# Weighting the experts' blocks two passes ahead, and fewer slots between the routing's steps

## The chip, the cores and the metric

The kernel runs on one core of one Trainium2 chip. The metric is the device time of one execution in microseconds (us), lower is better. The profile is of one execution on that core, taken by the hardware profiler; its time axis starts with the first instruction. Engines are named as the profile does: PE is TensorE (PEld its weight loads), DVE is VectorE, ACT is ScalarE, POOL is GpSimd, SP is SyncE, whose queue here issues most of the DMAs.

## The reference

Two layers run over x of shape (8, 384, 32, 32) in float32. Layer 0 adds a state space block (group norm, layer norm, projection, a short convolution, a selective scan over 1024 tokens with 16 states, gate, projection, and an MLP with Gelu). Layer 1, the one that the change touches, adds a mixture of four experts, and every expert is computed for every token:

```python
x_flat = x.transpose(0, 2, 3, 1).reshape(-1, c)
scores = softmax(x_flat @ gate_w + gate_b, -1)
top_v, top_i = jax.lax.top_k(scores, 2)
top_w = softmax(top_v, -1)
wmap = top_w.T.reshape(2, b, h, w)
present = (top_i[:, :, None] == jnp.arange(e)[None, None, :]).any(0)   # (2, E)
coef = jnp.einsum('ke,kbhw->ebhw', present, wmap)
hdn = relu(einsum('bchw,edc->ebdhw', x, w1) + b1)
y = einsum('ebdhw,eod->ebohw', hdn, w2) + b2
out = einsum('ebohw,ebhw->bohw', y, coef)          # x = x + out
```

Here x is the group-normed output of layer 0. `present` looks over all tokens at once: an expert counts as present at rank k if any token anywhere chose it there. So no coefficient is known before the last token has its scores. The second layer of an expert is linear, so the kernel may weight the hidden block by the coefficient ahead of it, and add coefficient times b2 to the sum.

## The kernel before

The tokens are cut into 16 chunks (`NCH`) of 512 (`T`); the 384 channels are 3 slabs (`J`) of 128 partitions. A hidden block of one expert and one chunk is 128 x 3 x 512.

**The first 3400 us** are the scan of layer 0 (loop L985), into which a planner fits everything else: the projections, the MLP, the scores of finished chunks, and the first expert layer (`expert_lane`, L606), which puts relu blocks through ACT into DRAM (`r_dram`).

**The planner.** All such work is written as generators that yield (engine, cost, wait). `wait` is the number of slots that must pass before the step after the yield may be issued; `Task.resume` (L792) sets `ready` to the current slot plus wait. `issue` (L801) takes ready steps by urgency (rank times 6, plus ready) until none is left. A step on "bank" also needs one of four PSUM banks, counted in `held`; an `evict` task frees it two slots later. The order in which the planner issues is the order of each engine's queue: each engine then works its queue off in that order, waiting on semaphores. In `drain` (L859) every slot issues all that is ready. So while the expert layer runs in a drain, a slot is worth some blocks of six matmuls (L619) on PE and as many evictions (L623) on ACT.

**The routing** (`route`, L629) starts when all 16 chunks have their logits (`logged`). It runs over all 64 token tiles at once, in steps, each after a yield with a wait: bias, maximum and subtraction on DVE (L649 to L651); Exp on ACT (L653); a long DVE step of softmax and of two rounds of picking the best (L655 to L679); a second Exp (L681) and its normalization (L683 to L685); a matmul over the counts, which is `present` (L690); the coefficients on DVE (L693 to L698); two transposes on PE (L705); a copy on ACT (L709); and two DMAs into `coef_dram` (L712). After the scan, `second_layers` (L867) begins `last_x1` and `route` with rank 0, ahead of all else, and drains until `routed`; then it fetches the coefficients of chunk 0 (L910) and drains the rest, which is the end of the first expert layer for the last chunk. Weight tiles of that layer come through `Stream`, three buffers, loaded by SP two blocks ahead (L218).

**The second expert layer** is the loop L913, one pass for each chunk and expert, 64 in all. There is no planner here: the order is that of the code. A pass tops up the list `ahead` of hidden blocks in flight (pool `phid`, six buffers, L894), at a chunk's first expert loads the next chunk's x1 (`load_sum`, L890, three buffers) and its coefficients, the same on all partitions (`load_coef`, L882, pool `pc`, two buffers, tile `spread`), and takes three accumulators, from `ps_acc` for even chunks and from the banks for odd ones. It multiplies the hidden block by its coefficients on DVE (L922), issues nine matmuls on PE (L925; each fp32 matmul is two instructions in the trace, so 18, and 72 for a chunk), and adds coefficient times bias to x1 on DVE, once for each slab (L928). At a chunk's last expert, `expert_out` (L897) adds the three accumulators to x1 on DVE (L900) and writes the result (L901). DVE and SP work strictly through what the passes have given them, so the first L922 of a chunk stands behind the three L900 of the chunk before.

Of the kernel before, what the change touches and what calls it, by code (L numbers as in the profile page):

```python
# [11 lines left out]
F32 = mybir.dt.float32  # L12
# [6 lines left out]
P = 128  # L19
B, C, L = 8, 384, 1024  # L20
T = 512
NH = L // T
NCH = B * NH
J = C // P
# [22 lines left out]
def chunk_of(dram, i):  # L47

    b, h = divmod(i, NH)
    return dram[b].rearrange("(p j) (n s) w -> n p j (s w)", p=P, n=NH)[h]  # L50


def wide(ap, shape):
    return ap.to_broadcast(shape)
# [56 lines left out]
def layers(ctx, tc, io, ident, cmean, eps, dram, x1_dram, gn1, logits, r_dram, group_norm):  # L111
# [9 lines left out]
    def pool(name, bufs, stack=ctx, **kw):  # L121
        return stack.enter_context(tc.tile_pool(name=name, bufs=bufs, **kw))
# [75 lines left out]
    def bank(name):  # L198
        held[0] += 1
        return ps_g.tile([P, T], F32, name=name, tag="g")  # L200

    def free():
        held[0] -= 1
# [394 lines left out]
    def last_x1(pool):  # L598
        while NCH - 1 not in scored:
            yield "-", 0, 1  # L600
        yield from normal_x1(NCH - 1, pool.tile([P, J, T], F32, name="last_xn"))
# [29 lines left out]
    def route(pool):  # L631
        while len(logged) < NCH:
            yield "-", 0, 1
        names = iter(range(99))

        def part(*shape):
            return pool.tile([P, *shape], F32, name=f"route{next(names)}")

        def over_experts(ap):
            return wide(ap.unsqueeze(2), [P, NT, E])  # L640

        def over_tiles(ap):
            return wide(ap.unsqueeze(1), [P, NT, E])

        yield "DVE", 2, 1
        ones = part(P)
        G.memset(ones, 1.0)
        sc, m = part(NT, E), part(NT)
        V.tensor_tensor(sc, logits, over_tiles(gate_b), ALU.add)  # L649
        V.tensor_reduce(m, sc, AX.X, ALU.max)  # L650
        V.tensor_tensor(sc, sc, over_experts(m), ALU.subtract)  # L651
        yield "ACT", 0.4, 2
        S.activation(sc, sc, AF.Exp)  # L653
        yield "DVE", 10, 0
        V.tensor_reduce(m, sc, AX.X, ALU.add)  # L655
        V.reciprocal(m, m)
        V.tensor_tensor(sc, sc, over_experts(m), ALU.mult)

        top = []
        count = part(2, E)  # L660
        for k in range(2):
            best = part(NT)
            V.tensor_reduce(best, sc, AX.X, ALU.max)
            pick = part(NT, E)
            V.tensor_tensor(pick, sc, over_experts(best), ALU.is_equal)

            left = part(NT)
            V.tensor_scalar(left, pick[:, :, 0], -1.0, 1.0, ALU.mult, ALU.add)
            for e in range(1, E):
                V.tensor_tensor(pick[:, :, e], pick[:, :, e], left, ALU.mult)  # L670
                V.tensor_tensor(left, left, pick[:, :, e], ALU.subtract)
            V.tensor_reduce(count[:, k, :], pick.rearrange("p t e -> p e t"), AX.X, ALU.add)
            if k == 0:
                V.scalar_tensor_tensor(sc, pick, -2.0, sc, ALU.mult, ALU.add)
            top.append(best)


        w_hi, w_lo = part(NT), part(NT)
        V.tensor_tensor(w_lo, top[1], top[0], ALU.subtract)  # L679
        yield "ACT", 0.3, 3  # L680
        S.activation(w_lo, w_lo, AF.Exp)  # L681
        yield "DVE", 1, 0
        V.tensor_scalar(w_hi, w_lo, 1.0, None, ALU.add)  # L683
        V.reciprocal(w_hi, w_hi)
        V.tensor_tensor(w_lo, w_lo, w_hi, ALU.mult)  # L685


        yield "bank", 0.2, 1
        total = bank("total")
        PE.matmul(total[:, 0:2 * E], lhsT=ones, rhs=count.rearrange("p k e -> p (k e)"), start=True, stop=True)  # L690
        yield "DVE", 1, 1
        present = part(2, E)
        V.tensor_scalar(present.rearrange("p k e -> p (k e)"), total[:, 0:2 * E], 0.5, None, ALU.is_gt)  # L693
        free()
        coef = part(NT, E)
        V.tensor_tensor(coef, over_experts(w_hi), over_tiles(present[:, 0, :]), ALU.mult)
        V.tensor_tensor(sc, over_experts(w_lo), over_tiles(present[:, 1, :]), ALU.mult)
        V.tensor_tensor(coef, coef, sc, ALU.add)  # L698


        half = NT // 2
        yield "bank", 0.4, 1
        ct = bank("ct")
        for k in range(2):
            PE.transpose(ct[:, k * P:(k + 1) * P], coef[:, k * half:(k + 1) * half, :].rearrange("p t e -> p (t e)"),  # L705
                         ident)
        yield "ACT", 0.4, 1
        cs = part(2, P)
        S.copy(cs, ct[:, 0:2 * P].rearrange("p (k n) -> p k n", k=2))  # L709
        free()  # L710
        for k in range(2):
            nc.sync.dma_start(coef_dram[k * half:(k + 1) * half].rearrange("t e s -> (t e) s"), cs[:, k, :])  # L712
        routed.append(True)
# [6 lines left out]
    def at(r):  # L720
        i, k = divmod(r, per)
        return i, *divmod(k, NG)
# [75 lines left out]
    def begin(*new, rank=2):  # L798
        tasks.extend(Task(t, rank) for t in new)
# [59 lines left out]
    def drain(until=lambda: not tasks):  # L859
        while not until():  # L860
            credit.update(PE=99, ACT=99, DVE=99, batch=99)
            issue(everything)
            slot[0] += 1
        credit.update(PE=0, ACT=0, DVE=0)


    def second_layers():  # L867
        def weight(name, shape):
            t = we.tile(shape, F32, name="w_" + name)
            nc.sync.dma_start(t, io[name])  # L870
            return t

        we, po, pc, px, phid = pool("we", 1), pool("po", 2), pool("pc", 2), pool("px", 3), pool("phid", 6)
        ps_acc = pool("ps_acc", 4, space=PSUM)
        todo = [(i, e) for i in range(NCH) for e in range(E)]
        spread = {}

        def load_coef(i):
            if i < NCH:
                spread[i] = pc.tile([P, TT, E, P], F32, name="spread")  # L880
                mine = coef_dram[i * TT:(i + 1) * TT]
                nc.sync.dma_start(spread[i].rearrange("p t e s -> p (t e s)"),  # L882
                                  mine.rearrange("t e s -> (t e s)").partition_broadcast(P))

        x2 = {}

        def load_sum(i):
            if i < NCH:
                x2[i] = px.tile([P, J, T], F32, name="x1")
                nc.sync.dma_start(x2[i], x1_dram[i])  # L890

        def load_hidden(n):
            (i, e), r = todo[n], phid.tile([P, J, T], F32, name="r")
            nc.sync.dma_start(r, r_dram[i][e * J:(e + 1) * J].rearrange("j p t -> p j t"))  # L894
            return r

        def expert_out(i, acc):  # L897
            o = po.tile([P, J, T], F32, name="o")
            for j in range(J):
                V.tensor_tensor(o[:, j, :], acc[j], x2[i][:, j, :], ALU.add)  # L900
            nc.sync.dma_start(chunk_of(io["out"], i), o)  # L901
            del x2[i]

        ahead = deque(load_hidden(n) for n in range(2))
        e2 = weight("e_w2", [P, E, J, J, P])
        eb2 = weight("e_b2", [P, E, J])
        load_sum(0)
        begin(last_x1(we), route(we), rank=0)
        drain(lambda: routed)
        load_coef(0)  # L910
        drain()

        for n in range(len(todo)):  # L913
            while len(ahead) < 4 and n + len(ahead) < len(todo):
                ahead.append(load_hidden(n + len(ahead)))
            (i, e), r = todo[n], ahead.popleft()
            if e == 0:
                load_sum(i + 1)
                load_coef(i + 1)
                acc = [ps_acc.tile([P, T], F32, name="acc") if i % 2 == 0 else bank("acc") for _ in range(J)]  # L920
            r4 = r.rearrange("p j (t s) -> p j t s", s=P)
            V.tensor_tensor(r4, r4, wide(spread[i][:, :, e, :].unsqueeze(1), [P, J, TT, P]), ALU.mult)  # L922
            for d in range(J):
                for j in range(J):
                    PE.matmul(acc[j], lhsT=e2[:, e, d, j, :], rhs=r[:, d, :], start=(e + d == 0), stop=(e + d == E + J - 2))  # L925
            for j in range(J):
                x4 = x2[i][:, j, :].rearrange("p (t s) -> p t s", s=P)
                V.scalar_tensor_tensor(x4, spread[i][:, :, e, :], eb2[:, e, j:j + 1], x4, ALU.mult, ALU.add)  # L928
            if e == E - 1:
                expert_out(i, acc)  # L930

    with tc.manual_schedule():
# [52 lines left out]
        for r in range(rounds):  # L985
            i, d, s = at(r)
# [75 lines left out]
```

## Time and profile before

| | |
|---|---|
| time, median of 3 runs (lowest to highest) | 4132.92 us (4128.94 to 4134.43) |
| time of the profiled execution | 4128.67 us |
| its span, first to last instruction | 4126.9 us |
| PE busy, share of the span | 3707.8 us, 90% |
| DVE busy | 3029.4 us, 73% |
| ACT busy | 2423.1 us, 59% |
| POOL busy | 2780.4 us, 67% |
| mean granted clock of TensorE | 0.951 |
| second expert layer, first matmul to the end of the last | 3576.34 to 4121.48 us |
| in it: PE busy, DVE busy, ACT busy | 508.3, 264.7, 0 us |
| DMA, mean over the span | 161 GB/s |

How it is read: a row of the timeline gives the start, the duration, the engine, the line of the kernel, the operation, what it writes and reads, how often, and in brackets how long the engine sat idle ahead of it and what ended that. The chain is followed back from the last instruction to what released each step, so time outside it did not set the end. Ends of matmuls are modelled, since they are pipelined: the start-to-start distance of weight loads is the surer measure of the pace. A granted clock of 1.00 is full speed.

### The profile page before, as it was taken

Reading aid. Unit: us, or ns where it says so; the run is one execution under the profiler, and the core shown is the slowest. Engines: PE = TensorE matmul, PEld = TensorE weight load, DVE = VectorE, ACT = ScalarE, POOL = GpSimd, SP = SyncE. Lnnn points to the kernel's source line nnn. Section 1 sums busy time; section 2 is a strip of 40 time slices with the busy share of each in tenths; the row PEclk is TensorE's granted clock in tenths of the full one; section 3 lists DMA queues with packets and bytes.
Section 4 is the critical chain, followed back from the end, with each engine's and each line's share of the span. In section 5 each row is a group of like instructions: output and inputs, shape, how many; then the busy total and the mean of one; then the engine's idle time right before and its main releaser. Section 6 shows DMA issues by size and latency. Waiting matters only on the chain. (4 is left out here: it accounts for less than half of the span.)

```text
span 4126.9 us, 35165 instructions
## 1 busy us (share of the span) xinstructions
PE 3707.8 (90%) x10294; PEld 1383.3 (34%) x10294; DVE 3029.4 (73%) x3081; ACT 2423.1 (59%) x3762; POOL 2780.4 (67%) x1070
## 2 busy tenths in 40 slices
PE   6678888999999999998999999999998998899998
PEld 2123223333333333333333333333333333344443
DVE  4888888888887888888878787888787770244444
ACT  4757676767676768676767676768666753100000
POOL 3898988788878888888888888888788860000000
PEclk8779898999999999999999999999999998999999
DMA  4434445464546454555455545554555443544443
GB/s 130 139 132 129 162 131 164 143 199 156 185 138 197 167 171 152 187 175 166 143 186 174 172 146 189 174 172 153 172 167 173 154 153 116 174 169 171 170 170 127
DMA packets 372499, 665.31 MB, mean 161 GB/s; under 512 B 40252, under 2 KB 151228, under 8 KB 370132
## 3 DMA queue, kind: packets, MB, share of 16 engines
q1 hardware_dynamic: 342496, 612.38, 44.8%
q10 hardware_dynamic: 29812, 50.68, 3.2%
q8 instruction: 83, 1.36, 0.1%
q14 instruction: 108, 0.88, 0.1%
HBM read 535.90 MB, written 127.01 MB: 161 GB/s over the span
## 5 line engine op out<-in xcount | busy, mean ns | idle before, releaser
L739 POOL TENSOR_TENSOR du<-dxr,b 128x2048 f32<-128x2048 f32 x384 | 1738.9, 4528 | 23.6 <-PE y L773 13.1
L751 POOL TENSOR_TENSOR du<-du,c 128x1024 f32<-128x1024 f32 x384 | 906.0, 2359 | 227.5 <-DVE du L747 202.2
L731 ACT ACTIVATE da_A<-dtr_a,w_a_log 128x512 f32<-128x512 f32 x768 | 527.6, 687 | 282.6 <-DVE du L751 123.1
L731 ACT ACTIVATE da_B<-dtr_b,w_a_log 128x512 f32<-128x512 f32 x768 | 527.3, 687 | 263.4 <-DVE du L747 210.7
L479 PE MATMUL hid<-tt,mlp_w 128*128 128x512 f32 x1152 | 535.9, 607 | 63.8 <-ACT h L483 46.7
L773 PE MATMUL y<-du,sel 128*32 128x512 f32 x3072 | 467.2, 641 | 130.2 <-DVE du L751 84.4
L747 DVE TENSOR_TENSOR_SCAN du<-da_B,carry,du 128x512 f32<-128x512 f32 x384 | 488.2, 1271 | 117.8 <-ACT da_B L731 109.9
L296 PE MATMUL g_in<-xt,in_proj 128*128 128x512 f32 x1152 | 556.8, 621 | 15.5 <-DVE x L523 8.4
L619 PE MATMUL e_hid<-xn,e_w 128*128 128x512 f32 x1080 | 517.9, 626 | 47.0 <-ACT r L623 25.7
L518 PE MATMUL acc<-h,mlp_w 128*128 128x512 f32 x1152 | 539.8, 611 | 22.4 <-ACT h L494 14.4
L747 DVE TENSOR_TENSOR_SCAN du<-da_B,du 128x512 f32<-128x512 f32 x384 | 464.5, 1210 | 122.1 <-ACT da_B L731 105.0
L925 PE MATMUL acc<-r,w_e_w 128*128 128x512 f32 x1152 | 508.3, 603 | 45.3 <-DVE r L922 40.3
L747 DVE TENSOR_TENSOR_SCAN da_A<-da_A,carry,du 128x512 f32<-128x512 f32 x384 | 489.1, 1274 | 8.6 <-ACT da_A L731 8.1
L747 DVE TENSOR_TENSOR_SCAN da_A<-da_A,du 128x512 f32<-128x512 f32 x384 | 465.5, 1212 | 27.6 <-ACT da_A L731 26.0
L751 DVE TENSOR_TENSOR du<-da_A,c 128x1024 f32<-128x1024 f32 x384 | 470.2, 1225 | 13.2
L479 PEld LDWEIGHTS hid<-tt,mlp_w 128*128 128x128 f32 x1152 | 213.9, 192 | 364.0 <-issue 236.3
L925 PEld LDWEIGHTS acc<-r,w_e_w 128*128 128x128 f32 x1152 | 221.6, 194 | 331.4 <-issue 277.5
L518 PEld LDWEIGHTS acc<-h,mlp_w 128*128 128x128 f32 x1152 | 215.5, 194 | 340.2 <-issue 247.9
L296 PEld LDWEIGHTS g_in<-xt,in_proj 128*128 128x128 f32 x1152 | 210.5, 194 | 354.0 <-issue 254.3
L619 PEld LDWEIGHTS e_hid<-xn,e_w 128*128 128x128 f32 x1080 | 207.0, 198 | 347.0 <-issue 247.9
L457 PE MATMUL g_out<-xc,out_proj 128*128 128x512 f32 x576 | 279.1, 632 | 32.0 <-DVE xc L780 32.0
L408 POOL TENSOR_TENSOR dtx<-dt,xc 128x512 f32<-128x512 f32 x96 | 122.1, 1272 | 209.9 <-DVE dt L405 209.8
(129 smaller groups left out, 3033.4 us busy)
## 6 DMA issues: line engine op xcount, KB each, us to landing
dxr<-dxr_dram SPq DMA_DIRECT2D x384, 256.0 KB, 4.8
mlp_w<-in_mlp_w SPq DMA_DIRECT2D x384, 192.0 KB, 3.2
dtr_b<-dtr_dram SPq DMA_DIRECT2D x192, 256.0 KB, 3.9
dtr_a<-dtr_dram SPq DMA_DIRECT2D x192, 256.0 KB, 3.2
r_dram<-r ACTq DMA_DIRECT2D x192, 256.0 KB, 3.3
r<-r_dram SPq DMA_DIRECT2D x64, 768.0 KB, 8.0
in_proj<-in_in_proj SPq DMA_DIRECT2D x192, 192.0 KB, 3.6
e_w<-in_e_w SPq DMA_DIRECT2D x192, 192.0 KB, 3.2
```

Source lines behind the costliest of these rows:

```text
L296: PE.matmul(g, lhsT=w[:, j, :], rhs=xt[i][:, j, :], start=(j == 0), stop=(j == J - 1))
L408: G.tensor_tensor(dtx, dt, xc[i, d], ALU.mult)
L457: PE.matmul(g, lhsT=w[:, d, :], rhs=xc[i, 3 * k + d], start=(k + d == 0), stop=(k == 1 and d == 2))
L479: PE.matmul(g, lhsT=w[:, j, :], rhs=tt[i][:, j, :], start=(j == 0), stop=(j == J - 1))
L518: PE.matmul(g, lhsT=w[:, n, :], rhs=hs[mine[n]], start=(k + n == 0), stop=(k == 1 and n == 2))
L619: PE.matmul(h, lhsT=w[:, j, :], rhs=xn[:, j, :], start=(j == 0), stop=(j == J - 1))
L731: S.activation(out, dtr[i, d][pair][:, j % 2, :], AF.Exp, scale=neg_a[:, d, j, s:s + 1])
L739: G.tensor_tensor(du[r], dxr[i, d], wide(bt[i, s].unsqueeze(1), [P, Q, T]), ALU.mult)
L747: V.tensor_tensor_scan(a if j < 2 else b, a, b, start, ALU.mult, ALU.add)
L751: engine.tensor_tensor(du[r][:, js, :], h, wide(ct[i, s].unsqueeze(1), [P, 2, T]), ALU.mult)
L773: PE.matmul(y[j * m:(j + 1) * m, :], lhsT=sel, rhs=h[:, j, :], start=False, stop=(s == NG - 1), tile_position=(0, j * m), skip_group_check ...
L925: PE.matmul(acc[j], lhsT=e2[:, e, d, j, :], rhs=r[:, d, :], start=(e + d == 0), stop=(e + d == E + J - 2))
```

## The change

In `route`, four waits become shorter by a slot each: the first DVE step 1 to 0 slots, the first Exp 2 to 1, the second Exp 3 to 2, the step on `total` 1 to 0. (The other waits stay.) In the second expert layer, what stood at the head of a pass, from topping up `ahead` to the weighting, becomes a function `weigh(n)`. It is called for passes 0 and 1 ahead of the loop, and for pass n + 2 in pass n, after the additions L928 and ahead of `expert_out`. The loads that hang on a chunk's first expert move with it. The accumulators are still taken in the pass that first uses them.

```diff
-        yield "DVE", 2, 1
+        yield "DVE", 2, 0
...
-        yield "ACT", 0.4, 2
+        yield "ACT", 0.4, 1
         S.activation(sc, sc, AF.Exp)
...
-        yield "ACT", 0.3, 3
+        yield "ACT", 0.3, 2
         S.activation(w_lo, w_lo, AF.Exp)
...
         PE.matmul(total[:, 0:2 * E], lhsT=ones, rhs=count.rearrange("p k e -> p (k e)"), start=True, stop=True)
-        yield "DVE", 1, 1
+        yield "DVE", 1, 0
         present = part(2, E)
...
-        for n in range(len(todo)):
+
+        weighted = {}
+
+        def weigh(n):
+            if n >= len(todo):
+                return
             while len(ahead) < 4 and n + len(ahead) < len(todo):
                 ahead.append(load_hidden(n + len(ahead)))
             (i, e), r = todo[n], ahead.popleft()
             if e == 0:
                 load_sum(i + 1)
                 load_coef(i + 1)
-                acc = [ps_acc.tile([P, T], F32, name="acc") if i % 2 == 0 else bank("acc") for _ in range(J)]
             r4 = r.rearrange("p j (t s) -> p j t s", s=P)
             V.tensor_tensor(r4, r4, wide(spread[i][:, :, e, :].unsqueeze(1), [P, J, TT, P]), ALU.mult)
+            weighted[n] = r
+
+        weigh(0)
+        weigh(1)
+        for n, (i, e) in enumerate(todo):
+            r = weighted.pop(n)
+            if e == 0:
+                acc = [ps_acc.tile([P, T], F32, name="acc") if i % 2 == 0 else bank("acc") for _ in range(J)]
             for d in range(J):
                 for j in range(J):
                     PE.matmul(acc[j], lhsT=e2[:, e, d, j, :], rhs=r[:, d, :], start=(e + d == 0), stop=(e + d == E + J - 2))
             for j in range(J):
                 x4 = x2[i][:, j, :].rearrange("p (t s) -> p t s", s=P)
                 V.scalar_tensor_tensor(x4, spread[i][:, :, e, :], eb2[:, e, j:j + 1], x4, ALU.mult, ALU.add)
+            weigh(n + 2)
             if e == E - 1:
                 expert_out(i, acc)
```

## Prediction

> **What bounds the kernel now.** I read four views. The chain that ended last, in order of time, comes first: it tells which of the changed lines set the end at all. The routing and the expert loop are its last part.
>
> ```profile
> 3557.26 10.40 PE e_hid L619 x24
> 3568.31 1.55 DMA coef_dram<-route
> 3569.87 4.53 DMA spread<-coef_dram
> 3574.53 1.77 DVE r L922
> 3576.34 33.18 PE acc L925 x72
> 3609.52 2.50 issue
> 3612.02 31.15 PE acc L925 x72
> 3643.80 1.76 DVE r L922
> 3645.60 32.69 PE acc L925 x72
> ```
>
> Columns: start, length, engine, tile, line. From 3576.34 to 4121.48 us the chain is TensorE on the 16 chunks (72 matmuls each), and between any two of them one weighting (L922) or an "issue" of the same length. Ahead of it stands the end of the routing: TensorE is done with e_hid at 3567.7 and idle until the coefficients are in DRAM, back on the chip, and the first block is weighted. Second, the timeline of VectorE at one boundary (start, length):
>
> ```profile
> 3641.48 0.69 DVE L900 TENSOR_TENSOR o<-acc,x 128x512 f32<-128x512 f32 x1 [16.61 <-PE acc L925]
> 3642.34 0.69 DVE L900 TENSOR_TENSOR o<-acc,x 128x512 f32<-128x512 f32 x1 [0.17 <-PE acc L925]
> 3643.19 0.69 DVE L900 TENSOR_TENSOR o<-acc,x 128x512 f32<-128x512 f32 x1 [0.17 <-PE acc L925]
> 3643.80 1.75 DVE L922 TENSOR_TENSOR r<-r,spread 128x1536 f32<-128x1536 f32 x1
> ```
>
> VectorE had been idle for 16.61 us, at the head of its queue an addition that waits for the accumulators. The next chunk's first weighting stands behind the additions, so TensorE waits for it. Third, the weight loads of TensorE after this boundary, and the windows of this chunk and the one before:
>
> ```profile
> 3645.60 0.50 PEld L925 LDWEIGHTS acc<-r,w_e_w 128*128 128x128 f32 x2 [3.28 <-DVE r L922]
> 3646.62 0.34 PEld L925 LDWEIGHTS acc<-r,w_e_w 128*128 128x128 f32 x1 [0.52 <-issue]
> ```
>
> ```profile
> 3612.00:3645.60 33.60, 31.14 (x72) 13.58 (x72) 16.66 (x20) 0.00 (x0) 0.00 (x0) 1.00 0.46 172
> 3645.60:3680.80 35.20, 32.70 (x73) 14.29 (x73) 16.75 (x20) 0.00 (x0) 0.00 (x0) 0.96 0.44 165
> ```
>
> After this gap a load takes 0.34 instead of 0.19 us and the pitch is 0.86 instead of 0.43: half clock, for some 3.4 us. The second window (columns: length, busy time of PE, PEld, DVE, ACT and POOL, then the granted clock, DMA share, GB/s) is 1.6 us longer, at clock 0.96. Fourth, the timeline of the routing:
>
> ```profile
> 3527.39 0.69 ACT L623 ACTIVATE r<-e_hid,w_e_b 128x512 f32<-128x512 f32 x1 [1.89 <-PE e_hid L619]
> 3536.20 0.42 ACT L653 ACTIVATE route<-route 128x256 f32<-128x256 f32 x1 [0.40 <-ACT r L623]
> 3545.68 0.26 ACT L681 ACTIVATE route<-route 128x64 f32<-128x64 f32 x1 [9.06 <-DVE route L679]
> 3546.57 10.57 PE L619 MATMUL e_hid<-last_xn,e_w 128*128 128x512 f32 x24 [1.19 <-ACT r L623]
> 3556.97 0.28 PE L690 MATMUL total<-route,route 128*128 128x8 f32 x2
> 3567.49 0.38 PE L705 MATMUL ct<-ident,route 128*128 128x128 f32 x2
> ```
>
> VectorE had the scores ready at 3521.4, but the first Exp ran at 3536.20: the planner had put it behind that many evictions. The transposes L705 stand behind the last e_hid block.
>
> [...] The half-clock stretches here start at 3645.60, 3747.99, 3850.36, 3952.75 and 4055.14, that is 102.4 us apart, [...] gaps of 2.45 us trip it, 5 of 15. [...]
>
> **The change, part by part.** All sums are against the profiled execution: 4128.67 us, span 4126.9, so 1.8 us lie around it. The median of the runs shown is 4132.92, 4.25 higher; I subtract from that.
>
> *1. Weighting two ahead.* No instruction is added: 64 weightings of 1.749 us and 192 additions of 0.744 us (L928) stay. A chunk's first two blocks are now weighted in the third and fourth pass of the chunk before, the second of them ahead of the additions L900. TensorE then has two blocks (18 matmuls each, 15.4 us) without VectorE. Behind the additions stand three L928 and a weighting (2.1 + 1.75 us), which are due 15.4 us after the boundary and done some 5.5 us after it: 10 us of cover. Start to start, an undisturbed chunk now takes 33.61 us (3612.02 to 3645.60); 72 matmuls at the steady pitch of the weight loads, 0.429 us, take 30.9. So a boundary costs 2.71[...], 15 of them 40.7 us.
>
> *2. Half clock.* Without gaps nothing trips it. The five long chunks take 35.15 instead of 33.61: 5 x 1.54 = 7.7 us. The first chunk takes 35.68, 2.07 more, after its 8.46 us of idle: gone as well if part 3 fills that. The stage goes from 545.1 (3576.34 to 4121.48) to 16 x 30.9 + 0.25 = 494.7: 50.5 us, the sum of the three.
>
> *3. Routing.* I follow the planner by hand; in the drain a slot issues all that is ready, and four banks bound the e_hid blocks. Counting from the slot in which the last logits are copied (0): before, the first VectorE step is in slot 2, the first Exp in 4, the second in 7, "total" tried in 8 and placed in 9 after eight blocks of the last chunk, transposes in 11 after all twelve, the copy in 12. That is the order the trace shows. After: VectorE step in 1, Exp in 2, second Exp in 4, "total" and the coefficients in 5, ahead of the last chunk's first block, transposes in 7 after its fourth, copy and the write of coef_dram in 8.
> Exp then runs behind the eviction of 3527.39, at about 3528.5, 7.7 us sooner; VectorE's 9 us of picks end at 3545.5 - 7.7 = 3537.8. "total" needs them, and TensorE reaches it at 3534.9, the end of the chunk before: a **new stall** of 3.0 us with all e_hid blocks queued behind it. In exchange the stall of 1.19 us at 3546.57 goes, for which the second Exp held ScalarE. Twelve blocks then run from 3538.1: 72 x 0.429 = 30.9, transposes 0.4, end 3569.4. Idle 3.0 us may trip the half clock: between 0 and 1.6, I take 0.8.
> On SP, in order, the write of coef_dram stands behind the weights of block 8, which wait for block 5's buffer: 3554. It lands 1.6 later; behind block 9's weights (3556.5) the coefficients are fetched: 4.5 us by the chain, 8.8 by the median landing of that row, so 3561 to 3565.4, and two weightings end at 3569 at the latest. The first is done by 3567.2, ahead of TensorE. If this cover failed, each us is one on the path. Weights of blocks 10 and 11, behind that fetch, are issued at 3559 and 3562, land 3.2 later, are used at 3564 and 3567: 2 us in hand.
> So the expert matmuls start at 3569.4 + 0.8 instead of 3576.3: 6.1 us.
>
> *4. Queues and buffers.* With each chunk's first weighting its loads move two blocks forward: x1 of the chunk after (a third buffer, free) and its spread. Spread has two buffers, and the older is read once more by L928 of the fourth block, so SP waits there until VectorE has passed it; VectorE runs ahead of TensorE, and that costs SP a few us. A block of r is now asked for five ahead in six buffers, so it waits for the block before the running one: 7.7 us each, landing 8.0, but four blocks early. The output's DMA holds SP until the additions are over, as before; the next r behind it is due over 20 us later. I take nothing for all this; if the cover were gone, a late r would cost up to its 8.0 us landing per chunk.
>
> Sum: 50.5 + 6.1 = 56.6 us. 4132.9 - 56.6 = **4076.3**; a profile near 4072.
>
> **The rivals.**
> - *The coefficients are late all the same* (one of the fetches or the stall is longer): part 3 gives nothing and the first chunk's 2.07 stay: 4132.9 - 48.4 = 4084.5. Against it: 2 us or more in hand. Chance 0.09.
> - *The half clock isn't tied to the gaps*: the 7.7 and 2.1 stay: 4086. For it: a period of 102.4 us. Against it: every stretch starts at the end of a gap, and three chunks make 102.4 as well. Chance 0.07.
> - *Another wait steps into the boundary* (spread or r after SP's new waits), half of the 40.7 stay, and of the 7.7: 4100. Chance 0.07.
> - *Transfers become the bound, slower.* A chunk moves 4 r, x1, spread and out: 5.77 MB. At 30.9 us that asks 187 GB/s; undisturbed chunks now move 172. If SP's waits let only the span's mean of 161 through, a chunk takes 35.8 us, the stage 573, and 4132.9 + 28 - 6 = 4155. It decides from 34.4 us per chunk (168 GB/s) on. Against it: 199 GB/s in a slice of the page, DMA shares under 0.5 in this stage. At 172 it would end near 4123. Chance 0.04.
> - *The change doesn't do what it says*: the planner would have to place the steps otherwise, or the old buffers hold the weighting back: 4133. Chance 0.01.
>
> **How the numbers follow.** The forecast has 0.72; its own spread is the half clock (0 to 1.6), the coefficients, and the 4 us between profile and median: 4070 to 4081. To 4087 the first two rivals are in: 0.88, less a little at the edges. Hence 4070 to 4087. A measurement of this kernel tells 0.2% (8 us) from no change; faster by more holds for all but the last two rivals: 0.95, same 0.02, slower 0.03.
>
> **What would show it.** Right: in the chain one run of acc matmuls without L922, chunk pitch 30.9, clock 1.00 throughout; L922 ahead of L900 on VectorE; Exp near 3528.5; "total" ahead of the last e_hid blocks, with some 3 us of idle before it; no idle before the first acc. Wrong: idle of TensorE with r, spread or x as releaser in the stage, half-clock loads with no gap before them, or a pitch over 31 us.

## The result and the profile after

| | before | after |
|---|---|---|
| median time, us (lowest to highest, runs) | 4131.88 (4128.94 to 4134.43, 4) | 4077.61 (4072.95 to 4086.60, 4) |
| span of the profiled execution | 4126.9 | 4073.9 |
| first DVE step of the routing (L649) to the end | 606.8 | 551.1 |
| second expert layer, first matmul to the end of the last | 545.1 | 494.6 |

The ratio of the times is 0.9872, 95% interval 0.9853 to 0.9890: 1.3% faster, 54.3 us (45 to 61 by the interval). The forecast was 4076.3 us, which is 56.6 us less.

The third row needs a word. Up to L649 no instruction is changed, yet the ten profiles of this study reach it between 3512.0 and 3531.7 us. Executions of one kernel scatter nearly as much: 15 runs of the kernel before spread over 15.2 us. This scatter is larger than some of the effects below. So each profile is measured from its own L649 to its end. There the change saves 55.8 us; the spans, 53.0 us apart, hold 2.8 us of that scatter.

The end of the chain that ended last, after (start, length, engine, tile, line, count):

```profile
3541.14 12.10 PE e_hid L619 x24
3553.46 20.60 PE e_hid L619 x48
3574.06 494.41 PE acc L937 x1152
4068.50 0.69 DVE o L900
```

All 16 chunks are one unbroken run of TensorE, 1152 matmuls of 0.429 us; no weighting and no "issue" stands between them, and e_hid runs straight into them. (The timeline, which the table uses, counts this run from its first start, 3573.90, and gives it 494.56 us.) VectorE at the first boundary, in the timeline of after:

```profile
3587.90 1.75 DVE L926 TENSOR_TENSOR r<-r,spread 128x1536 f32<-128x1536 f32 x1
...
3603.28 0.69 DVE L900 TENSOR_TENSOR o<-acc,x 128x512 f32<-128x512 f32 x1 [13.63 <-PE acc L937]
3604.14 0.69 DVE L900 TENSOR_TENSOR o<-acc,x 128x512 f32<-128x512 f32 x1 [0.17 <-PE acc L937]
3605.00 0.69 DVE L900 TENSOR_TENSOR o<-acc,x 128x512 f32<-128x512 f32 x1 [0.17 <-PE acc L937]
3605.61 2.07 DVE L940 SCALAR_TENSOR_TENSOR x<-spread,w_e_b,x 128x512 f32<-128x512 f32 x3
...
3607.59 1.75 DVE L926 TENSOR_TENSOR r<-r,spread 128x1536 f32<-128x1536 f32 x1
```

VectorE still idles ahead of the additions (13.63 us here), but the next chunk's second weighting starts over 15 us before them. The weighting behind them ends at 3609.3, and its block is the third of the new chunk, which TensorE reaches some 11 us later. The windows (length, busy time of PE, PEld, DVE, ACT and POOL, granted clock, DMA share, GB/s) show the clock and the traffic:

```profile
3600.00:3700.00 100.00, 100.00 (x234) 44.31 (x233) 53.77 (x63) 0.00 (x0) 0.00 (x0) 1.00 0.51 180
3700.00:3800.00 100.00, 100.00 (x234) 44.28 (x233) 57.39 (x66) 0.00 (x0) 0.00 (x0) 1.00 0.54 189
```

TensorE is busy throughout, at clock 1.00; the DMA engines carry 180 to 189 GB/s in about half of their time. The routing, in the timeline of after:

```profile
3530.18 0.69 ACT L623 ACTIVATE r<-e_hid,w_e_b 128x512 f32<-128x512 f32 x1 [1.89 <-PE e_hid L619]
3531.33 0.42 ACT L653 ACTIVATE route<-route 128x256 f32<-128x256 f32 x1 [0.46 <-ACT r L623]
3540.78 0.36 PE L690 MATMUL total<-route,route 128*128 128x8 f32 x2 [2.92 <-DVE route L679]
3541.00 12.24 PE L619 MATMUL e_hid<-last_xn,e_w 128*128 128x512 f32 x24
3553.08 0.38 PE L705 MATMUL ct<-ident,route 128*128 128x128 f32 x2
3561.64 0.38 SPq L882 DMA_DIRECT2D spread<-coef_dram  x1
3567.54 3.43 DVE L926 TENSOR_TENSOR r<-r,spread 128x1536 f32<-128x1536 f32 x2 [24.08 <-DMA r_dram<-r]
```

Exp runs 8.5 us after L649, where it took 16.1 before. The count matmul L690 now stands ahead of the last chunk's twelve blocks, and TensorE waits 2.92 us for the picks (L679) that it needs. The 24 matmuls behind it take 12.24 us instead of some 10.4. Both weightings of the first blocks end by 3570.97, 2.9 us ahead of TensorE at 3573.90. (The last row names a write of r to DRAM as releaser, which the weighting does not read. Of what it does read, the spread was fetched last, at 3561.64, 5.9 us earlier.)

### The profile page after: what moved, and what is told of

It reads as the page before. It is cut to its first block, busy times and chain, and to the rows that moved or that the text cites. A ratio compares the mean times of both kernels' runs of the same rounds, so it can differ in the third digit from the quotient of the medians.

```text
span 4073.9 us, 35181 instructions
## 1 busy us (share of the span) xinstructions
PE 3697.5 (91%) x10294; PEld 1383.9 (34%) x10294; DVE 3030.1 (74%) x3081; ACT 2422.4 (59%) x3762; POOL 2779.7 (68%) x1070
## 5 line engine op out<-in xcount | busy, mean ns | idle before, releaser
L937 PE MATMUL acc<-r,w_e_w 128*128 128x512 f32 x1152 | 494.6, 592 | 0.0
```

## The experiments

The explanation to be tested has three parts: the breaks of TensorE at 15 boundaries (40.7 us), the half clock that some of them set off (7.7 us), and the gap ahead of the stage (the rest). In the table, "from L649" is the profile's time from there to the end, and "saved" is against before's 606.8. There is one profile of each kernel, so these have no interval; but after, e3 and e4, whose TensorE does the same work in the same order, agree to 0.5 us. The ratio of after is to the 4 runs of the kernel before shown above, those of e1 to e4 are to 15 further runs of it (median 4130.97), and those of e5 to e8 to 7 (4129.23).

| kernel | median, us | ratio, 95% interval | from L649, us | saved, us |
|---|---|---|---|---|
| after | 4077.61 | 0.9872 (0.9853 to 0.9890) | 551.1 | 55.8 |
| e1_loop_only | 4079.83 | 0.9883 (0.9858 to 0.9908) | 558.3 | 48.6 |
| e2_route_only | 4128.43 | 0.9989 (0.9978 to 1.0000) | 600.3 | 6.5 |
| e3_one_ahead | 4075.50 | 0.9872 (0.9857 to 0.9887) | 551.5 | 55.3 |
| e4_adds_first | 4074.07 | 0.9866 (0.9850 to 0.9883) | 551.1 | 55.7 |
| e5_by_slab | 4106.24 | 0.9950 (0.9935 to 0.9965) | 582.7 | 24.2 |
| e8_bias_first | 4180.97 | 1.0127 (1.0112 to 1.0142) | 661.2 | -54.4 |
| e6_total_later | 4073.20 | 0.9869 (0.9849 to 0.9890) | 548.6 | 58.3 |
| e7_coef_act | 4074.68 | 0.9875 (0.9860 to 0.9890) | 547.4 | 59.4 |

**The two halves of the change.** e1 is the kernel after with the four old waits, e2 the kernel before with the four new ones:

```diff
 e1, against after (e2, against before, has the same four lines the other way)
-        yield "DVE", 2, 0
+        yield "DVE", 2, 1
...
-        yield "ACT", 0.4, 1
+        yield "ACT", 0.4, 2
...
-        yield "ACT", 0.3, 2
+        yield "ACT", 0.3, 3
...
-        yield "DVE", 1, 0
+        yield "DVE", 1, 1
```

> The new expert loop with the routing's old waits. Theory (boundaries 40.7 us, half clock 7.7 us, routing the rest): the stage keeps its idle of 8.5 us ahead of the first matmul and the slow first chunk (2.1 us), then runs at a pitch of 30.9 us; 48.4 us saved, 4083.5 us. Rival (the earlier coefficients are what lets the loop run ahead): waits for r or spread in the first chunks, over 4090 us.

> The shorter waits with the old expert loop. Theory: the gap of 8.5 us ahead of the stage goes, a stall of 2.9 us at the count matmul comes, the first chunk runs at full clock; the 15 boundaries stay as they were: 5.1 + 2.1 = 7 us saved, 4125 us. Rival (routing worth nothing, its gain is given back): 4132 us.

The timeline of TensorE in e1 has the stage as one row:

```profile
3568.37 496.45 PE L937 MATMUL acc<-r,w_e_w 128*128 128x512 f32 x1152 [8.52 <-DVE r L926]
```

The 8.52 us ahead of it are still there, and it is 1.9 us longer than after's 494.56, which is the slow start behind that idle. No wait for r or spread appears, so the loop does not need the earlier coefficients. 48.6 us are saved from L649, and 51 by the medians (38 to 59 by their interval); 48.4 were expected. In e2 the first rows of the stage are

```profile
3583.32 31.06 PE L925 MATMUL acc<-r,w_e_w 128*128 128x512 f32 x72
3616.87 31.14 PE L925 MATMUL acc<-r,w_e_w 128*128 128x512 f32 x72 [2.49 <-issue]
```

with no idle ahead of the first one and the boundaries as they were. Its profile saves 6.5 us from L649. The medians, 2.5 us apart, agree with that only as far as their interval reaches (0 to 9 us): the size of this half is read from the profile. The two halves make 55.1 of 55.8 us, so they add up.

**How far ahead, and ahead of what?**

```diff
 e3, against after
         weigh(0)
-        weigh(1)
...
-            weigh(n + 2)
+            weigh(n + 1)
```

```diff
 e4, against after
-            weigh(n + 2)
             if e == E - 1:
                 expert_out(i, acc)
+            weigh(n + 2)
```

> As after, but weighted one pass ahead, still in front of the additions. Theory: one block (7.7 us of TensorE) covers the additions, the bias additions and the next weighting (done 5.3 us after the boundary): no gap, 4077.6 us like after. Rival (two blocks are needed): gaps at the boundaries, pitch over 31 us, 4085 us or more.

> As after, two passes ahead, but the weighting behind the additions. Theory: the next chunk's first block is weighted one pass earlier anyway, the second is due 7.7 us after the boundary and done some 3.5 us after it: no gap, 4077.6 us like after. Rival (the place in front of the additions is what counts): a gap at each boundary, 4100 us or more.

Both do what after does: TensorE runs through the 16 chunks without a break, in 494.56 us. In e3 the block behind the additions is the new chunk's second; in e4 the additions stand ahead of that same weighting, as its timeline shows:

```profile
3600.02 0.69 DVE L900 TENSOR_TENSOR o<-acc,x 128x512 f32<-128x512 f32 x1 [16.03 <-PE acc L937]
...
3602.34 1.75 DVE L926 TENSOR_TENSOR r<-r,spread 128x1536 f32<-128x1536 f32 x1
```

This weighting ends at 3604.1, and TensorE needs it 7.7 us after the boundary at about 3601.7. So the change does one thing twice: what counts is that one weighted block is in hand when the additions wait. The second pass ahead, or the place in front, is spare.

**Is the half clock set off by the gaps?** In the kernel before, the half clock came every 102.4 us, which is both three chunks and 30 times 3.413 us, the length of each of the five stretches at its boundaries in the trace; these two kernels tell them apart.

```diff
 e5, against before
-            V.tensor_tensor(r4, r4, wide(spread[i][:, :, e, :].unsqueeze(1), [P, J, TT, P]), ALU.mult)
+            if e == 0:
+                for j in range(J):
+                    V.tensor_tensor(r4[:, j], r4[:, j], spread[i][:, :, e, :], ALU.mult)
+            else:
+                V.tensor_tensor(r4, r4, wide(spread[i][:, :, e, :].unsqueeze(1), [P, J, TT, P]), ALU.mult)
```

```diff
 e8, against before (bias holds the three additions of L928)
+            if e == 0:
+                bias(i, e)
             V.tensor_tensor(r4, r4, wide(spread[i][:, :, e, :].unsqueeze(1), [P, J, TT, P]), ALU.mult)
...
-            for j in range(J):
-                x4 = x2[i][:, j, :].rearrange("p (t s) -> p t s", s=P)
-                V.scalar_tensor_tensor(x4, spread[i][:, :, e, :], eb2[:, e, j:j + 1], x4, ALU.mult, ALU.add)
+            if e > 0:
+                bias(i, e)
```

> The kernel before, with a chunk's first weighting cut into three slabs of 128x512, so that TensorE starts after the first. Theory (half clock is set off by idle time[...]): idle at a boundary falls from 2.45 to 1.4 us, and no chunk but the first runs at half clock: 15.9 + 7.7 = 24 us saved, 4108 us. Rival (the half clock comes every 102.4 us whatever the gaps): five slow stretches stay, 4116 us.

> The kernel before, with a chunk's first three bias additions put ahead of its first weighting: 2.07 us more idle at each boundary, nothing else. Theory: with 4.5 us of idle every one of the 15 boundaries sets off the half clock (1.5 to 2.1 us each): 31 + 2 + 15 to 20, about 4180 us. Rival (every 102.4 us whatever the gaps): 33 us more, 4165 us.

TensorE's timeline of e5:

```profile
3706.58 31.17 PE L929 MATMUL acc<-r,w_e_w 128*128 128x512 f32 x72 [1.38 <-DVE r L924]
3739.13 31.17 PE L929 MATMUL acc<-r,w_e_w 128*128 128x512 f32 x72 [1.38 <-DVE r L924]
```

and of e8:

```profile
3653.93 32.86 PE L932 MATMUL acc<-r,w_e_w 128*128 128x512 f32 x72 [4.44 <-DVE r L929]
3691.27 33.38 PE L932 MATMUL acc<-r,w_e_w 128*128 128x512 f32 x72 [4.48 <-issue]
```

with the slow weight loads at the head of the second:

```profile
3692.26 0.33 PEld L932 LDWEIGHTS acc<-r,w_e_w 128*128 128x128 f32 x1 [0.52 <-issue]
```

With 1.4 us of idle none of the 15 boundaries is followed by a long chunk, with 2.45 five are (in before, and in e2 too), with 4.4 all 15. The long chunks of e8 take 1.7 and 2.2 us more than 31.17, in turn (the first of them 2.3). The half clock is the price of the gaps, and the period is an accident of their spacing. Both times are near what was expected: from L649, 24.2 us saved (24 expected) and 54.4 lost (48 to 53 expected); by the medians 23.0 and 51.7.

Which gaps set it off can be worked out too. The traces record when the granted clock changed, and in each profile every stretch of half clock starts on one grid of 3.413 us (58 stretches in before and 56 in after, all within 0.01 us of it). Split each gap at the lines of this grid: none with at most 1.95 us of idle in any one interval was followed by half clock, and each with 1.97 us or more in one was. This holds at all 60 boundaries of before, e2, e5 and e8, and for the gaps from the count matmul to the head of the stage in the other kernels (the two nearest to the limit are the 1.95 us of e6 and the 1.97 us of e4). In before, every third gap lies almost whole in one interval, with 2.14 to 2.20 us in it; the other ten have at most 1.68. That is why 2.45 us do it one time in three. In e8 the gaps that cost 2.2 us have over 2 us in two intervals in a row, those that cost 1.7 in one only. (The start of a gap is the modelled end of a matmul, so the limit is no more exact than these ends.)

**A version without the new stall.**

```diff
 e6, against after
-        yield "bank", 0.2, 1
+        yield "bank", 0.2, 2
         total = bank("total")
```

```diff
 e7, against e6
-            nc.sync.dma_start(coef_dram[k * half:(k + 1) * half].rearrange("t e s -> (t e) s"), cs[:, k, :])
+            S.dma_start(coef_dram[k * half:(k + 1) * half].rearrange("t e s -> (t e) s"), cs[:, k, :])
...
-                nc.sync.dma_start(spread[i].rearrange("p t e s -> p (t e s)"),
+                (S if i == 0 else nc.sync).dma_start(spread[i].rearrange("p t e s -> p (t e s)"),
```

> As after, but the count matmul one slot later (its wait 1 to 2), so that it stands behind four blocks of the last chunk, and the transposes behind eight. Theory: the stall of 2.9 us and the half clock behind it (1.8 us) go, but the write of the coefficients now stands on SP behind the last weights (block 11's, due when block 8 is done): the first weighting ends 1 to 2 us after TensorE's last e_hid block; 3 us less than after, 4074.6 us. Rival (the later coefficients cost more than the stall): 4080 us.

> As e6_total_later, with the write of the coefficients and the fetch of chunk 0's on ScalarE's queue, right behind the copy that they need. Theory: no stall, no half clock, the first weighting done ahead of TensorE: 4.7 us less than after, 4073 us. Rival (ScalarE held for the landing of the write, some 2 us, makes the evictions late): like after, 4077.6 us.

In the timeline of e6 the stall and the slow matmuls behind it are gone, but the coefficients are late:

```profile
3547.68 0.28 PE L690 MATMUL total<-route,route 128*128 128x8 f32 x2
3547.82 10.55 PE L619 MATMUL e_hid<-last_xn,e_w 128*128 128x512 f32 x24
...
3570.94 14.43 PE L937 MATMUL acc<-r,w_e_w 128*128 128x512 f32 x33 [2.06 <-DVE r L926]
```

In e7 that last idle is 0.92 us. Its write goes out at 3561.97, right behind the copy, and its fetch at 3563.70, but that fetch takes 6.25 us in the chain where e6 has 5.04. ScalarE is held 2.22 us for the landing of the write, but TensorE does not idle behind it until the first matmul of the stage:

```profile
3571.89 13.57 PE L937 MATMUL acc<-r,w_e_w 128*128 128x512 f32 x31 [0.92 <-DVE r L926]
```

From L649 they are 2.5 and 3.7 us shorter than after (3.0 and 4.7 expected). The medians of after, e6 and e7 can't be told apart: their intervals overlap almost wholly. By its one profile e7 is the best of these kernels; by the measured times that isn't shown.

## Why the prediction was right

*Part 1 and 2.* The stage was to shrink by 50.5 us, to 494.7; it shrank by 50.6, to 494.6. The price of a boundary as start-to-start 33.61 against 72 pitches, 2.71 and not the idle 2.45, was the right one: 15 times the difference is 4 us. (The profile gives the 72 matmuls of an undisturbed chunk 31.17 us, some 0.3 over 72 pitches: on the page of before the record of one lasts 603 ns on average, and the next starts after 429.) That the half clock goes with the gaps was only inferred from its place; e5 and e8 show it. That not every gap of 2.45 us sets it off was taken as found, without a reason; the grid above gives one.

*Part 3.* The planner's order worked out by hand is the order of the trace. The stall was forecast at 3.0 us and is 2.92 (3.04 in e2). The half clock behind it was taken at 0.8, half of its bound, as if it might not come; it came in all four kernels that have the stall (after, e2, e3, e4), and cost about 1.8 us, above the 1.6 given as the upper end. So the expert matmuls start 5.2 us earlier, counted from L649, instead of 6.1 (55.8 less the stage's 50.6). This is the one term of the sum that was mis-sized. The fetch was set at 3556.5; with after's offset of 2.8 and the half clock's 1.8 that is 3561.1, and it went out at 3561.64. The "2 us in hand" of the last weights was too good: these loads took up to 5.2 us rather than 3.2, and in e2 and e3 the last twelve or so e_hid matmuls wait for them at the edge, as this piece of e2's timeline shows:

```profile
3578.09 5.39 PE L619 MATMUL e_hid<-last_xn,e_w 128*128 128x512 f32 x12 [0.18 <-DMA e_w<-in_e_w]
```

It costs 0.18 us. In these two kernels the chain runs through this load, so nothing of the 2 us was left; in after it does not.

*Part 4.* SP does wait, as said: 280 us for r behind TensorE in the stage of after, the longest 7.3. None of it reaches TensorE. For the buffer of spread, where a wait of SP was forecast too, the profile names none. Transfers as the bound are refuted: 187 GB/s were asked for, and 180 to 199 are seen in full windows of 100 us, at a DMA share of at most 0.57; the first 26 us of the stage even move 321 GB/s, at a share of 0.84. (The rival's side sum, 4123 at 172 GB/s, comes out near 4118 when the routing's 6 us are taken off, as in its 4155.) Of the other rivals, late coefficients and another wait at the boundary are refuted by the unbroken chain.

*The number.* 54.3 us by the medians against 56.6: 0.9 us is part 3, and the other 1.4 us are within the scatter of the runs. From L649 the profile saves 55.8, so all but 0.8 us is there. That the time itself comes nearer, 4077.61 against 4076.3, is luck: the forecast subtracts from the first median, 4132.92, which a fourth run lowered by 1.0 us.

## What to carry to other kernels

An engine that works its queue off in order, as VectorE did in before (idle for 16.6 to 18.6 us ahead of each chunk's additions, with the next weighting behind them), and is about to wait for a result, should already have passed on the next piece of work to whoever produces that result. One piece is enough if it lasts longer than everything that stands between the wait and the piece after it: here the piece is 7.7 us of TensorE, and VectorE had the next one ready about 4.5 us (e3) and 2.5 us (e4) after the boundary. Price a gap on TensorE from start to start against its steady pitch, and add the half clock: here 1.4 us of idle was free of it, and 2.45 us set it off one time in three, when it lay so that about 2 us of it fell into one interval of 3.4 us. When a step is moved forward in a planner, ask when its inputs are ready at the new place: here the moved count matmul became a stall of 3 us with a slow stretch behind it.

## What the runs showed that was not expected

The identical code ahead of the routing took between 3512 and 3532 us in ten profiles. By the records of the granted clock, half clock was in force for 358 us of it in the shortest (e1) and for 399 us in the longest (e2). If TensorE had worked throughout these 41 us, about 20 us would be lost in them (an estimate), and 19.7 is the difference. Over all ten profiles the two go together, though loosely in the middle (correlation 0.9). So stretches of half clock that fall differently on many short gaps fit the scatter; but longer idle time for another reason would bring more half clock with it, no run here separates the two, and it stays open.
